# A message-passing layer: one tile in eighteen takes its source rows from x on chip, column by column, and not by a gather

## The chip, the cores and the metric

The kernel runs on one core of a Trainium2 chip. A core has five engines with a queue of instructions each: PE (matrix products), DVE (vector operations), ACT (activations and copies), POOL (here it only issues the gathers) and SP (issues DMAs). They run in parallel and wait for each other through semaphores; within a queue the order is fixed. PE, DVE and ACT work on 128 partitions of the on-chip memory; a product is accumulated in PSUM. The metric is the device time of one execution in microseconds (us), smaller being better; the median of several executions counts.

## The reference

One graph layer with a residual and a normalisation, on 12,500 nodes of 64 features and 200,000 edges of 32 features, all float32. The edges are sorted by `dst`; `src` is random.

```python
def _mlp(x, W1, b1, W2, b2):
    return jax.nn.relu(x @ W1 + b1) @ W2 + b2
msg_in = jnp.concatenate([nodes[row], nodes[col], edge_features], axis=-1)   # 64 + 64 + 32
messages = _mlp(msg_in, mW1, mb1, mW2, mb2)                                  # 160 -> 128 -> 64
aggregated = jax.ops.segment_sum(messages, col, num_segments=nodes.shape[0])
upd_in = jnp.concatenate([nodes, aggregated], axis=-1)
return _mlp(upd_in, uW1, ub1, uW2, ub2)                                      # 128 -> 128 -> 64
...
x = _layernorm(x + _L0_gnn_ref(x, src, dst, ...), axis=-1)
```

`row` is `src` and `col` is `dst`. The part of this page is the hidden layer of the message: relu(x[src] W1a + x[dst] W1b + e W1c + b1), where W1a, W1b and W1c are the three row blocks of mW1.

## The kernel before

**Tables.** x[src] W1a depends on the node alone. So the kernel first multiplies all of x with W1a and with W1b (plus b1) and writes two tables of 12,544 x 128 floats to HBM: A (`tab_a`, `chunk_a`) and B (`tab_b`, `chunk_b`). For an edge the hidden layer is then a row of A at its source, plus a row of B at its destination, plus the edge's own part.

**Tiles and groups.** 128 edges are a tile; there are 1563. Six tiles (`SUB`) are a group, s; there are 261. Twelve tiles, two groups, (`SUP`) share the selection matrices. The loop from line 583 handles group s in each turn and issues for several groups ahead.

**What a group needs.**
- `gather` (line 157): POOL issues one indirect DMA a tile (line 168). It fetches 128 rows of 512 bytes of A, at the indices in `src_s`, into one of 18 buffers `xg` (`ROWB`). So POOL runs up to 18 groups ahead and waits until DVE has read the buffer it wants (`frees`). The first ten groups (`XG`) gather rows of x instead, which PE transposes and multiplies with `w1a` (lines 231 and 270), since A is not ready yet.
- `windows` (line 217): the edges are sorted by destination, so a tile's destinations lie within 32 neighbouring nodes. SP loads six values from `wint` into registers (line 224) and issues six DMAs, each of 32 rows of B at a register's offset, into `rhs` (line 229).
- `loadd` and `load` (lines 177 and 211): SP loads the destinations (line 184) and the edge features (line 215) of two groups into `l`.
- `select` (line 187): DVE turns the destinations into zeros and ones that pick rows of the window (line 196), and into `sel`, which sums the edges into nodes (line 200).
- `edge_part` (line 246): PE multiplies [edge features; selection] with [W1c; window of B] in one product a tile (line 256), two passes each.
- `node_part` (line 260): DVE adds the gathered rows to the product (line 276), ACT applies the relu (line 277).
- `collect` (line 287): PE multiplies the result with the selection, at a column offset from a register (loaded at line 298), which sums the edges by node (line 302); a second product counts the edges (line 307).

At 33 points, 47 groups apart at first and four at the end, a block of nodes is complete: `update`, `residual`, `norm` and `store` (lines 333 to 370) compute the second layers and the normalisation and write the output. `rest` (line 504) issues some loads of the first groups; `columns` (line 326) loads x of a block of nodes.

**Order.** It is written out by hand. In turn s each engine gets, in this order: the gathers that have become possible, `windows(s + 2)`, `node_part(s)`, `collect(s - 1)`, in even turns `select` and `load`, in odd turns `loadd`, then `edge_part(s + 1)`. So in ACT's queue the relu of group s + 1 stands behind all that ACT gets in turn s, and on DVE the add at line 276 of group s + 1 stands behind the selections of turn s. The matrix products of group s + 1 stand on PE behind `collect(s - 1)`, which waits for the relu of group s - 1.

Of the kernel before, what the change touches and what calls it, by code (L numbers as in the profile page):

```python
# [10 lines left out]
F32 = mybir.dt.float32  # L11
I32 = mybir.dt.int32
AF = mybir.ActivationFunctionType
ALU = mybir.AluOpType
AX = mybir.AxisListType
ET = mybir.EngineType

P = 128
N, D, DE, DH = 12500, 64, 32, 128
E = 200000  # L20
EPS = 1e-5
NB = -(-N // P)
NPAD = NB * P
NT = -(-E // P)
SUB = 6
SUP = 12
NSUP = -(-NT // SUP)
NTP = NSUP * SUP
EPAD = NTP * P
NSUB = -(-NT // SUB)  # L30
# [7 lines left out]
XG = 10  # L38
# [2 lines left out]
EARLY = NCH * P  # L41
GE = 26
BS = 11
UB = 4
NCOL = (-(-N // P) + UB) * P
UN = 448
# [17 lines left out]


@with_exitstack
def gnn_kernel(ctx: ExitStack, tc: tile.TileContext, x1T, x, eT, e_rows, src, dst, dst_row, wrow, wnext, whalf,
               mW1, mb1, mW2, mb2, uW1, ub1, uW2, ub2, out):

# [20 lines left out]
    nc = tc.nc  # L92
    const = ctx.enter_context(tc.tile_pool(name="const", bufs=1))
# [7 lines left out]
    K = len(UPD)  # L101

    src_s = const.tile([P, NT], I32, name="src_s")
    wint = const.tile([1, NTP], I32, name="wint")
    past = const.tile([1, 1], F32, name="past")

    xall = const.tile([P, -(-NB // NCH), HB * P], F32, name="xall")
# [8 lines left out]
    w1a = const.tile([P, DH], F32, name="w1a")  # L116
# [19 lines left out]
    slot = cps[:, :WIN]  # L136
# [1 line left out]
    flag_i = const.tile([1, 1], I32, name="flag_i")  # L138
    usup = const.tile([1, K], I32, name="usup")
    ustep = const.tile([1, K], I32, name="ustep")  # L140
    woff = const.tile([1, NTP], I32, name="woff")
    wh = const.tile([P, NTP // 2], I32, name="wh")
    wa = const.tile([SUP, NSUP], I32, name="wa")
    wb = const.tile([SUP, NSUP], I32, name="wb")
# [9 lines left out]
    def tiles(s):  # L154
        return range(s * SUB, min((s + 1) * SUB, NT))

    def gather(s):

        if s >= XG or s % 2 == 0:
            buf = rows.tile([P, SUB, DH], F32, name="xg")  # L160
        else:
            buf = xg[s - 1][0]
        if s < XG:
            a = buf.rearrange("p k (b d) -> p (k b) d", d=D)[:, s % 2 * SUB:(s % 2 + 1) * SUB, :]
        else:
            a = buf.rearrange("p (b k) d -> p k b d", b=2)
        for i, t in enumerate(tiles(s)):
            nc.gpsimd.indirect_dma_start(  # L168
                out=a[:, i, :] if s < XG else a[:, i // 2, i % 2, :], out_offset=None, in_=A[:, :] if s >= XG else x[:, :],
                in_offset=bass.IndirectOffsetOnAxis(ap=src_s[:, t:t + 1], axis=0))  # L170
        xg[s] = buf, a

    with tc.tile_pool(name="sup", bufs=2) as sup, tc.tile_pool(name="work", bufs=2) as work, tc.manual_schedule():
# [66 lines left out]
        def parts(n):  # L240

            if n == SUB:
                return [(slice(0, 2), SUB // 2)]
            return [(slice(b, b + 1), (n - b + 1) // 2) for b in range(2) if n > b]

        def edge_part(s):

            n = len(tiles(s))
            g, j = divmod(s, SUP // SUB)

            pc = psum.tile([P, 2, 4, DH], F32, name="pc")[:, :, :SUB // 2]
            for i in range(n):
                k, b = divmod(i, 2)
                q, m = 64 * b, j * SUB // 2 + k

                nc.tensor.matmul(pc[:, b, k, :], L[g][q:q + 64, m, :], rhs[g % 2][q:q + 64, m, :],  # L256
                                 start=s >= XG or k == 0, stop=s >= XG)
            pcs[s] = pc

        def node_part(s):  # L260

            n = len(tiles(s))
            pc = pcs.pop(s)
            h = work.tile([P, 2, SUB // 2, DH], F32, name="h")
            if s < XG:
                xt = xs.pop(s)
                for i in range(n):
                    k, b = divmod(i, 2)
                    q = 64 * b
                    nc.tensor.matmul(pc[:, b, k, :], xt[q:q + 64, k, :], w1a[q:q + 64], start=False,  # L270
                                     stop=i + 2 >= n)
                nc.scalar.activation(h, pc, AF.Relu)
            else:
                a = xg.pop(s)[0].rearrange("p (b k) f -> p b k f", b=2)
                for b, m in parts(n):
                    nc.vector.tensor_tensor(h[:, b, :m], pc[:, b, :m], a[:, b, :m], op=ALU.add)  # L276
                    nc.scalar.activation(h[:, b, :m], h[:, b, :m], AF.Relu)  # L277
            hs[s] = h

        def opened(u):  # L280
# [37 lines left out]
        def close(u):  # L318

            ps, pn = sums.pop(u)  # L320
            nc.scalar.copy(sums_s[u % 2], ps)  # L321
            nc.scalar.copy(xw[u % 2][0:1, :UW], pn)

        us = {}

# [15 lines left out]
        def residual(u):  # L341

            n0 = us[u]
            py = psum.tile([P, UB, D], F32, name="py", tag="pc")
            for i in range(UB):
# [29 lines left out]
        def relative(a, b):  # L375

            wbc = work.tile([P, WCH], I32, name="wbc", tag="tb")
            nc.sync.dma_start(dst_s[:, a:b], dst[:, a:b])
            nc.sync.dma_start(wbc[:, :b - a], wrow[:, a:b].broadcast_to([P, b - a]))
            nc.vector.tensor_tensor(drc[:, a:b], dst_s[:, a:b], wbc[:, :b - a], op=ALU.subtract)  # L380
# [43 lines left out]
        def chunk_b(c, into):  # L424
            pb, tb = products(c, w1b)
            n = min(NCH, NB - c)
            pf, tf = (t.rearrange("p h i f -> p (h i) f")[:, :n] for t in (pb, tb))
            nc.vector.tensor_tensor(tf, pf, b1.unsqueeze(1).broadcast_to([P, n, DH]), op=ALU.add)
            for v in into:
                nc.sync.dma_start(v[:, c:c + n, :], tf)  # L430
# [53 lines left out]
        for k, c in enumerate(range(0, NB, NCH)):  # L484
# [14 lines left out]
            if k == 9:  # L499
                select(0)  # L500
                load(0)
                counts(0)

        def rest(s):

            if s == 1:
                relative(8 * SUP, 8 * SUP + WCH)
            elif s == 2:
                relative(8 * SUP + WCH, NT)
                halves(4 * SUP, NTP // 2)  # L510
            elif s == BS:
                nc.sync.dma_start(wa, wrow.rearrange("o (p c) -> (o p) c", c=NSUP))
                nc.sync.dma_start(wb, wnext.rearrange("o (p c) -> (o p) c", c=NSUP))
                nc.scalar.dma_start(w2, mW2)
                nc.scalar.dma_start(u1a, uW1[D:2 * D, :])
                nc.scalar.dma_start(b2c, mb2.rearrange("(f o) -> f o", o=1))
                nc.vector.memset(uz[:D], 0.0)
                nc.vector.memset(ux[:D], 0.0)
                nc.vector.memset(eps, EPS)
                nc.vector.memset(ones, 1.0)  # L520
                nc.vector.tensor_copy(ux[D:], ident[D:, D:])
                nc.scalar.dma_start(uz[D:], uW1[0:D, :])
                nc.scalar.dma_start(ux[ONE:ONE + 1], ub2.rearrange("(o f) -> o f", o=1))
                nc.scalar.dma_start(ub1_s, ub1.rearrange("(f o) -> f o", o=1))
                nc.scalar.dma_start(u2, uW2)
            elif s == BS + 2:
                weights()
                checks()
# [54 lines left out]
        for s in range(last + 3):  # L583
            g, j = divmod(s, SUP // SUB)
            while gathered < NSUB and frees(gathered) < s:
                gather(gathered)
                gathered += 1
            if s - 2 in due:
                norm(due[s - 2])
            if s + 2 < NSUB:  # L590
                windows(s + 2)
            if s < NSUB:
                node_part(s)
            if 1 <= s <= NSUB:
                collect(s - 1)
            if s + 1 in due:
                close(due[s + 1])
            if j == 0 and g + 1 < NSUP:
                select(g + 1)
                load(g + 1)  # L600
                counts(g + 1)
            if j == 1 and g + 2 < NSUP:
                loadd(g + 2)
            if chunks and s >= BS and chunks[0] < NCH + NB * (s + 1 - BS) / (SUP // SUB * (GE - 1) - BS):
                chunk_b(chunks.pop(0), [Bv])
            if s + 1 < NSUB:
                if s + 1 < XG:
                    transpose(s + 1)
                edge_part(s + 1)
            if s in due and due[s] + 1 < K:  # L610
                carry(due[s] + 1)
            if s in due:
                update(due[s])
            if s - 1 in due:
                residual(due[s - 1])
            if s + 2 in due:
                columns(due[s + 2])
            rest(s)
            if s - 2 in due:
                store(due[s - 2])  # L620
# [3 lines left out]
                          skip_runtime_bounds_check_because="a count of edges")  # L624
    with tc.If(flag > 0), tc.tile_pool(name="gen", bufs=1) as up:
# [28 lines left out]
        with tc.For_i(0, NT, 1) as t:  # L654
# [26 lines left out]
            pc = psum.tile([P, DH], F32, name="pcg", tag="pc")  # L681
# [4 lines left out]
            h = up.tile([P, DH], F32, name="hg")  # L686
# [6 lines left out]
            m = up.tile([P, 1], F32, name="m")  # L693
# [22 lines left out]
        with tc.For_i(0, NB, 1) as c:  # L716
# [24 lines left out]
            o = up.tile([P, D], F32, name="o")  # L741
# [45 lines left out]
```

## Time and profile before

| | us |
|---|---|
| median of 6 runs | 2753.09 (2743.26 to 2767.78) |
| the profiled execution, its own time | 2757.78 |
| its span in the profile | 2756.0 |
| gathers of A: issuing time on POOL, 1503 instructions | 1417.9 |
| edge products (line 256), 3126 passes on PE | 575.2 |
| collecting products (line 302), 3126 passes on PE | 685.3 |
| DVE, the add of the gathered rows (line 276), 252 | 238.8 |
| ACT, the relu (line 277), 252 | 210.9 |

A row of the profile's groups reads: line, engine, operation, what it writes <- what it reads, count | busy time, mean duration in ns | idle time of the engine before it, and what ended most of that. "issue" means that nothing the profile shows was waited for. SPq, PEldq and the like are instructions of an engine's sequencer (register loads, waits, DMA issues), which do not count as busy. In the order of time a line begins with the start and the length in us, and merges like instructions that follow each other.

### The profile page before, as it was taken

To read this page: it belongs to the slowest core of one execution; us is meant where nothing else is said; L and a number is where in the kernel's file an instruction comes from. 1 tells how busy PE (TensorE), PEld (TensorE's weight loads), DVE (VectorE), ACT (ScalarE), POOL (GpSimd) and SP (SyncE) were. 2 spreads that over 40 slices of the span, in tenths; PEclk is the share of its full clock that TensorE was granted. 3 is DMA by queue.
4 is the path that set the end of the run, shared out by engine and by line. 5 is a ranking of instruction groups with operands and counts; after the bars stand their busy time and mean duration, and the time that the engine had idled before them with its cause. 6 is when DMAs were issued, how large, how long until landed. Compare 5 with 4: busy or idle time off the path is not lost. (4 is left out here: it accounts for less than half of the span.)

```text
span 2756.0 us, 34854 instructions
## 1 busy us (share of the span) xinstructions
PE 1651.5 (60%) x9218; PEld 1410.1 (51%) x9218; DVE 551.7 (20%) x1165; ACT 359.0 (13%) x550; POOL 1475.7 (54%) x1572
## 2 busy tenths in 40 slices
PE   1413556666656565656666565665656575676798
PEld 1312555555555455545555554554555464564576
DVE  0200122221212112112212112121222122121233
ACT  0100111111111111111111111111111111111122
POOL 7175455656555656565655555555555555556400
PEclk7555555555555555555555555555555555555555
DMA  5421233333222222222222222222223222222221
GB/s 122 125 74 49 67 80 86 87 98 83 75 71 70 76 73 73 70 74 72 76 75 75 71 66 74 75 75 72 75 73 78 74 74 74 75 77 71 73 58 44
DMA packets 244062, 208.45 MB, mean 76 GB/s; under 512 B 78232, under 2 KB 208369, under 8 KB 243874
## 3 DMA queue, kind: packets, MB, share of 16 engines
q0 software_dynamic: 50016, 100.57, 14.7%
q1 hardware_dynamic: 179312, 96.69, 12.7%
q10 hardware_dynamic: 14546, 8.93, 1.1%
q8 instruction: 88, 1.44, 0.2%
q14 instruction: 100, 0.82, 0.1%
HBM read 188.25 MB, written 17.69 MB: 75 GB/s over the span
## 5 line engine op out<-in xcount | busy, mean ns | idle before, releaser
L168 POOL DMA_INDIRECT xg<-tab_a,src_s x1503 | 1417.9, 943 | 1128.2 <-issue 415.1
L256 PE MATMUL pc<-rhs,l 64*128 64x128 f32 x3126 | 575.2, 444 | 737.6 <-DMA l<-in_eT 441.8
L256 PEld LDWEIGHTS pc<-rhs,l 64*128 64x128 f32 x3126 | 457.2, 312 | 815.1 <-issue 658.6
L302 PEld LDWEIGHTS sums<-sel,h 128*128 128x128 f32 x3126 | 670.6, 318 | 158.3 <-issue 141.5
L302 PE MATMUL sums<-sel,h 128*128 128x32 f32 x3126 | 685.3, 386 | 93.8 <-issue 81.2
L276 DVE TENSOR_TENSOR h<-pc,xg 128x768 f32<-128x768 f32 x252 | 238.8, 949 | 990.0 <-issue 684.6
L277 ACT ACTIVATE h<-h 128x768 f32<-128x768 f32 x252 | 210.9, 837 | 876.6 <-DVE h L276 617.8
L196 DVE TENSOR_TENSOR l<-l,cps 128x768 f32<-128x768 int32 (+1 forms) x134 | 127.9, 954 | 545.1 <-DMA l<-in_dst_row 509.9
L208 ACT CAST selb<-sel 128x384 bf16<-128x384 f32 x131 | 66.7, 509 | 742.7 <-remote 262.2
L307 PE MATMUL cnt<-selb,one 128*1 128x32 bf16 x1563 | 96.7, 188 | 61.6 <-issue 61.3
L200 DVE TENSOR_TENSOR sel<-cps,drc 128x384 f32<-128x384 f32 x131 | 72.1, 550 | 237.0 <-remote 167.6
L307 PEld LDWEIGHTS <-one 128*1 128x1 bf16 x1563 | 58.1, 83 | 114.2 <-issue 99.5
L346 PE MATMUL py<-ux,xw 128*128 128x64 f32 x264 | 78.1, 394 | 5.7 <-ACT hTu L339 4.7
L347 PE MATMUL py<-u,hTu 128*128 128x64 f32 x264 | 76.7, 388 | 2.2 <-issue 1.6
L410 PE MATMUL pb<-w1a,xall 64*128 64x128 f32 x196 | 25.3, 432 | 85.1 <-DVE tb L418 59.5
L351 DVE BATCH_NORM_STATS2 st<-py 128x6 f32<-128x64 f32 x132 | 20.6, 218 | 258.6 <-PE py L347 231.8
L346 PEld LDWEIGHTS py<-ux,xw 128*128 128x128 f32 x264 | 63.9, 297 | 13.9 <-issue 7.1
L410 PEld LDWEIGHTS pb<-w1a,xall 64*128 64x128 f32 x196 | 22.6, 324 | 87.4 <-DVE tb L418 61.3
L168 POOL DMA_INDIRECT xg<-in_x,src_s x60 | 56.8, 946 | 19.2 <-issue 18.0
L347 PEld LDWEIGHTS py<-u,hTu 128*128 128x128 f32 x264 | 65.1, 301 | 2.0 <-issue 1.3
L337 PE MATMUL pu<-sums_s,w2u 128*128 128x448 f32 x66 | 61.5, 1035 | 0.5 <-ACT sums_s L321 0.5
L338 PE MATMUL pu<-xw,uz 128*128 128x448 f32 x66 | 55.1, 938 | 0.0
(87 smaller groups left out, 440.4 us busy)
## 6 DMA issues: line engine op xcount, KB each, us to landing
l<-in_dst_row SPq DMA_DIRECT2D x262, 96.0 KB
l<-in_eT SPq DMA_DIRECT2D x262, 96.0 KB
rhs<-tab_b SPq DMA_DIRECT2D x1563, 16.0 KB
xg<-tab_a,src_s POOLq DMA_INDIRECT x1503
tab_b<-tb SPq DMA_DIRECT2D x13, 512.0 KB
tab_a<-tb ACTq DMA_DIRECT2D x12, 512.0 KB
out<-o SPq DMA_DIRECT2D x33, 128.0 KB
xw<-in_x1T SPq DMA_DIRECT2D x33, 113.8 KB
```

What stands on the lines that cost most here:

```text
L168: nc.gpsimd.indirect_dma_start(out=a[:, i, :] if s < XG else a[:, i // 2, i % 2, :], out_offset=None, in_=A[:, :] if s >= XG else x[:, :], ...
L196: nc.vector.tensor_tensor(l[r], l[r].bitcast(I32), node[r].unsqueeze(2).broadcast_to([r.stop - r.start, SUP // 2, P]), op=ALU.is_equal)
L200: nc.vector.tensor_tensor(s[:, :nt], slot.unsqueeze(1).broadcast_to([P, nt, WIN]), drc[:, g * SUP:g * SUP + nt].unsqueeze(2).broadcast_to( ...
L208: nc.scalar.copy(sb[:, :nt], S[g][:, :nt])
L256: nc.tensor.matmul(pc[:, b, k, :], L[g][q:q + 64, m, :], rhs[g % 2][q:q + 64, m, :], start=s >= XG or k == 0, stop=s >= XG)
L276: nc.vector.tensor_tensor(h[:, b, :m], pc[:, b, :m], a[:, b, :m], op=ALU.add)
L277: nc.scalar.activation(h[:, b, :m], h[:, b, :m], AF.Relu)
L302: nc.tensor.matmul(ps[:, bass.ds(ws[i], WIN)], h[:, i % 2, i // 2, :], S[g][:, k0 + i, :], start=False, stop=ends and i == n - 1)
L307: nc.tensor.matmul(pn[:, bass.ds(ws[i], WIN)], one, SB[g][:, k0 + i, :], start=False, stop=ends and i == n - 1)
L337: nc.tensor.matmul(pu, w2u, sums_s[u % 2][:, :UN], start=True, stop=False)
L346: nc.tensor.matmul(py[:, i], xw[u % 2][:, i * P:(i + 1) * P], ux, start=True, stop=False)
L347: nc.tensor.matmul(py[:, i], hT[:, i * P:(i + 1) * P], u2, start=False, stop=True)
```

## The change

In one of each three groups from group 20 on, the sixth tile is no longer gathered. The kernel now keeps x, transposed, on chip (`xcol`: 64 partitions, a column of 12,544 nodes), loaded by seven DMAs in turns 3 to 9 (`rest`). For each of the 128 edges of such a tile, one instruction copies the 64 values of its source's column into a column of a 128-column tile `xo`. The column's offset comes from a register, which is loaded from `srow`, a table of the sources of these tiles. The copies are spread over three turns (`copies`, called before `edge_part(s + 1)`): of 42 or 43 columns a turn, ACT copies 24, by two register loads of twelve, and DVE the rest, as an addition of a PSUM value that is zero. PE then multiplies `xo` with `w1a` into the tile's product. In `node_part` of such a group the add covers five of six tiles, and the relu is two instructions: one of the sixth tile from PSUM, one of the rest. `wint` and `woff` now lie in the unused partition 0 of `xcol`.

```diff
+CG = 3
+CF = 6 * CG
+CA = 24
+    def copied(s):
+        return s >= CF and s % CG == CG - 1 and len(tiles(s)) == SUB
     def gather(s):
...
-        for i, t in enumerate(tiles(s)):
+        for i, t in enumerate(tiles(s)[:SUB - copied(s)]):
...
     def edge_part(s):
...
+                c = copied(s) and i == n - 1
                 nc.tensor.matmul(pc[:, b, k, :], L[g][q:q + 64, m, :], rhs[g % 2][q:q + 64, m, :],
-                                 start=s >= XG or k == 0, stop=s >= XG)
+                                 start=s >= XG or k == 0, stop=s >= XG and not c)
+                if c:
+                    nc.tensor.matmul(pc[:, b, k, :], xo[s // CG % 2][q:q + 64], w1a[q:q + 64], start=False, stop=True)
...
     def node_part(s):
...
+                if copied(s):
+                    for b, m in ((0, SUB // 2), (1, SUB // 2 - 1)):
+                        nc.vector.tensor_tensor(h[:, b, :m], pc[:, b, :m], a[:, b, :m], op=ALU.add)
+                    hf = h.rearrange("p b k f -> p (b k) f")
+                    nc.scalar.activation(hf[:, SUB - 1], pc[:, 1, SUB // 2 - 1], AF.Relu)
+                    nc.scalar.activation(hf[:, :SUB - 1], hf[:, :SUB - 1], AF.Relu)
...
+        def copies(s):
+            q, i = divmod(s + 2, CG)
+            t = q * CG + CG - 1
+            if t < CF or not t < NSUB or not copied(t):
+                return
+            k, e = i * P // CG, (i + 1) * P // CG
+            r = q - CF // CG
+            to = xo[q % 2]
+            def by_dve(o, i):
+                nc.vector.tensor_tensor(o, i, slot[D:, 0:1], op=ALU.add)
+            parts = []
+            for a, b, en, copy in ((k, k + CA // 2, ET.Activation, nc.scalar.copy),
+                                   (k + CA // 2, k + CA, ET.Activation, nc.scalar.copy),
+                                   (k + CA, e, ET.DVE, by_dve)):
+                _, v = nc.values_load_multi_w_load_instructions(
+                    srow[r:r + 1, a:b], engines=[en], min_val=0, max_val=N - 1,
...
+                parts += [(copy, a + i, v[i]) for i in range(b - a)]
+            for copy, i, v in parts:
+                copy(to[D:, i:i + 1], xcol[D:, bass.ds(v, 1)])
...
         def rest(s):
+            if 3 <= s and (s - 3) * XCH < NB * P:
+                c = (s - 3) * XCH
+                e = min(c + XCH, NB * P)
+                nc.sync.dma_start(xcol[D:, c:e], x1T[1:, c:e])
...
+                nc.sync.dma_start(srow, src_row[CF * SUB + SUB * CG - 1::SUB * CG, :][:NCT])
...
+            copies(s)
             if s + 1 < NSUB:
```

More of the change, by code (lines that the diff above doesn't have):

```diff
@@ L43 @@
 BS = 11
+CG = 3
+CF = 6 * CG
+CA = 24
+NCT = -(-(NSUB - CF) // CG)
 UB = 4
@@ L66, in gnn_kernel @@
 @with_exitstack
-def gnn_kernel(ctx: ExitStack, tc: tile.TileContext, x1T, x, eT, e_rows, src, dst, dst_row, wrow, wnext, whalf,
+def gnn_kernel(ctx: ExitStack, tc: tile.TileContext, x1T, x, eT, e_rows, src, src_row, dst, dst_row, wrow, wnext, whalf,
                mW1, mb1, mW2, mb2, uW1, ub1, uW2, ub2, out):
@@ L103, in gnn_kernel @@
     src_s = const.tile([P, NT], I32, name="src_s")
-    wint = const.tile([1, NTP], I32, name="wint")
+    xcol = const.tile([P, NB * P], F32, name="xcol")
+    wint, woff = (xcol[0:1, k * NTP:(k + 1) * NTP].bitcast(I32) for k in range(2))
+    srow = const.tile([NCT, P], I32, name="srow")
+    xo = [const.tile([P, P], F32, name=f"xo{k}") for k in range(2)]
     past = const.tile([1, 1], F32, name="past")
@@ L140, in gnn_kernel @@
     ustep = const.tile([1, K], I32, name="ustep")
-    woff = const.tile([1, NTP], I32, name="woff")
     wh = const.tile([P, NTP // 2], I32, name="wh")
@@ L274, in node_part @@
                 a = xg.pop(s)[0].rearrange("p (b k) f -> p b k f", b=2)
-                for b, m in parts(n):
-                    nc.vector.tensor_tensor(h[:, b, :m], pc[:, b, :m], a[:, b, :m], op=ALU.add)
-                    nc.scalar.activation(h[:, b, :m], h[:, b, :m], AF.Relu)
+                if copied(s):
[4 more added lines that the diff above has]
+                    nc.scalar.activation(hf[:, :SUB - 1], hf[:, :SUB - 1], AF.Relu)
+                else:
+                    for b, m in parts(n):
+                        nc.vector.tensor_tensor(h[:, b, :m], pc[:, b, :m], a[:, b, :m], op=ALU.add)
+                        nc.scalar.activation(h[:, b, :m], h[:, b, :m], AF.Relu)
             hs[s] = h
@@ L322, in close @@
             nc.scalar.copy(xw[u % 2][0:1, :UW], pn)
+        def copies(s):
[14 more added lines that the diff above has]
+                    srow[r:r + 1, a:b], engines=[en], min_val=0, max_val=N - 1,
+                    skip_runtime_bounds_check_because="sources are node numbers")
+                parts += [(copy, a + i, v[i]) for i in range(b - a)]
+            for copy, i, v in parts:
+                copy(to[D:, i:i + 1], xcol[D:, bass.ds(v, 1)])
         us = {}
@@ L502, in gnn_kernel @@
                 counts(0)
+        XCH = 2048
         def rest(s):
+            if 3 <= s and (s - 3) * XCH < NB * P:
+                c = (s - 3) * XCH
+                e = min(c + XCH, NB * P)
+                nc.sync.dma_start(xcol[D:, c:e], x1T[1:, c:e])
             if s == 1:
@@ L769 @@
         "src": sp.reshape(-1, P).T[:, :NT],
+        "src_row": sp.reshape(-1, P),
         "dst": dp[:EPAD].reshape(-1, P).T[:, :NT],
```

## The prediction

> **What bounds the kernel now.** I read the table of busy time first, to see whether one engine is full.
>
> ```profile
> PE 1651.5 (60%) x9218; PEld 1410.1 (51%) x9218; DVE 551.7 (20%) x1165; ACT 359.0 (13%) x550; POOL 1475.7 (54%) x1572
> ```
>
> None is. ACT and DVE, which get the new work, are the idlest. Next the pace, from the stages view over the even middle of the run (engines in the order PE, PEld, DVE, ACT, POOL; then granted clock, DMA share, GB/s):
>
> ```profile
> 500.00:2500.00 2000.00, 1241.35 (x6771) 1060.39 (x6770) 406.02 (x824) 266.97 (x404) 1141.88 (x1211) 0.51 0.29 75
> ```
>
> 1211 gathers are 201.8 groups of six, so a group takes 2000/201.8 = 9.91 us. ACT works 1.32 us of that and DVE 2.01 us. Then the order of time, for POOL and for SP's queue:
>
> ```profile
> 1504.65 3.12 SPq L229 DMA_DIRECT2D rhs<-tab_b  x6
> 1506.51 0.94 POOL L168 DMA_INDIRECT xg<-tab_a,src_s  x1 [4.10 <-DVE cps L194]
> 1507.76 0.94 POOL L168 DMA_INDIRECT xg<-tab_a,src_s  x1 [0.31 <-issue]
> ...
> 1509.95 13.44 SPq L229 DMA_DIRECT2D rhs<-tab_b  x6
> ...
> 1520.25 0.94 POOL L168 DMA_INDIRECT xg<-tab_a,src_s  x1 [0.30 <-issue]
> ...
> 1525.75 3.09 SPq L229 DMA_DIRECT2D rhs<-tab_b  x6
> ...
> 1535.00 0.94 POOL L168 DMA_INDIRECT xg<-tab_a,src_s  x1 [13.81 <-DVE cps L194]
> ```
>
> Gathers start 1.25 us apart (1506.51 to 1507.76), mostly twelve in a row. The six window loads of a group take SP 3.1 us when no gather runs, and 13.4 us while gathers flow, from about 3.4 us after a run's start to 2.2 us after its end: SP nearly halts. The engines that need SP's loads then wait, and POOL in its turn waits for a buffer that DVE frees late. The list of waits confirms both directions:
>
> ```profile
> DVE l L196 <- DMA l<-in_dst_row: 509.9, 98, 12.3
> PE pc L256 <- DMA l<-in_eT: 441.8, 78, 13.3
> POOL xg L168 <- DVE h L276: 326.3, 77, 10.4
> POOL xg L168 <- DVE cps L194: 286.8, 57, 16.0
> ```
>
> So gathers and the rest take turns. PE's clock (0.51) matters little: PE idles 38% here. PE too is halted late in a run of gathers, one instruction at a time, for no reason the trace names:
>
> ```profile
> 1549.15 0.28 PEld L256 LDWEIGHTS pc<-rhs,l 64*128 64x128 f32 x1 [1.12 <-issue]
> 1549.85 0.37 PE L256 MATMUL pc<-rhs,l 64*128 64x128 f32 x1 [1.04 <-issue]
> ```
>
> Whether ACT and DVE are halted as well this trace cannot tell: they issue only a handful of instructions in such a stretch.
>
> **What is removed.** Copied tiles are those of groups 20, 23, ... 257: 80 gathers of 1563. At 1.25 us that is 100 us at most (if the gather runs set the pace) and 0 at least (if SP's own issuing does).
>
> **What is added.** The copies are spread over 240 groups: 128 columns per three groups, of which ACT takes 24 in each group and DVE 18.67 on average. No row shows such an instruction; the nearest are these (durations in ns: least, median, greatest):
>
> ```profile
> L355 ACT ACTIVATE sd<-mv,eps x33: 297/297/298, 703.4 to 2750.1; 128x4 f32<-128x4 f32 x33
> L298 PEldq TENSOR_LOAD <-woff x261: 776/1124/1806, 132.7 to 2737.6; - x131
> L312 PEldq TENSOR_LOAD <-ustep x32: 302/308/321, 689.3 to 2725.5; - x32
> L307 PEldq FUSED_REGOPS  x1563: 37/37/37, 134.6 to 2741.8; - x196
> 109.63 0.13 DVE L445 COPY usup<-wint 1x1 int32<-1x1 int32 x1
> ```
>
> ACT, per group:
> - Copies: a small ACT instruction lasts 0.297 us, and neighbours overlap by 0.10 (L277 at 1514.74 starts 0.53 us after L339, which lasts 0.63). That is 0.20 from start to start, and 24 x 0.20 = 4.80 us. The register operation ahead of each (0.037 us) hides under the copy before it; uncovered it would be 0.9 us.
> - Register loads: one value takes 0.308 us, six take 1.124 (median), so a further value costs 0.163. Twelve values take 0.308 + 11 x 0.163 = 2.10 us, two such loads 4.20. They stand ahead of all the copies, so ACT runs dry behind them. By the least of six values (0.776) it would be 2 x 1.34 = 2.68; if ACT's queue covers them wholly, 0. I take the medians, because a load in a crowded stretch is what happens here.
> - The relu of a copied group becomes two: by L355 (4 columns, 0.297) and L277 (768, 0.837), 0.39 + 0.75 less 0.10 of overlap is 0.2 more, every third group: under 0.10.
> - With its present 1.32 this makes 1.32 + 4.80 + 4.20 + 0.10 = 10.42 us, against a pace of 9.91. ACT becomes the engine that sets the pace.
>
> The Trainium skill's page "Runtime: NRT & Kernel Launch", section on instruction fetch, speaks against the change more strongly: about 200 ns for each register loaded. The slope between the two rows above is 163 ns. By the page's figure, an estimate, two loads of twelve would cost 4.8 us and ACT 11.0 us a group, some 145 us more over the run than by the rows.
>
> DVE, per group: 2.01 + one load of 18.67 values (0.308 + 17.67 x 0.163 = 3.19) + 18.67 copies x 0.17 (L445 to its successor at 109.80) = 3.17, in all 8.4 us, under the pace. But they come after the selection and ahead of the next L276, so that add, the relu behind it and the buffer it frees for POOL wait up to 6.4 us longer. Slack of 1.5 us a group hides them; without it they would cost the same as ACT's excess.
>
> PE: two passes more per copied tile, 160 matmuls at 0.18 (twelve take 2.1 us at 1525.54), 28 us, hidden in PE's idle time; 0 to 28, I take 0. Its new wait for the copied columns holds up the collecting matmuls behind it, but the copies are ordered one whole group earlier, so it costs nothing unless ACT falls a group behind.
>
> SP: eight more DMAs ahead of group 10. At about 0.4 us to issue (L330's median is 0.372) 3 us; the 3.2 MB at 158 GB/s (the best stage) 20 us if nothing hides it. SP's rows queue behind it. 0 to 23; I take 5, since the DMA share there is a quarter.
>
> **Sum.** ACT's excess 240 x (10.42 - 9.91) = 122 us, plus 5: 2757.8 + 127 = 2885. The removed 100 us are not subtracted, because POOL then waits for ACT's pace. The sum is against the profiled execution (2757.8, span 2756.0 plus 1.8 around it), 4.7 over the median of the six, 2753.1; I state 2885. Its own range: 2770 when half of the loads is covered, 3150 when ACT keeps half of its present wait for L276 (617.8/252 = 2.45 us, so 1.2 x 240 = 290 on top).
>
> **Rival: the copies are hidden, faster.** ACT's and DVE's idle time is 8.6 and 7.9 us a group, and their sequencers can load registers while the engine still works off its queue. Without the loads ACT needs 6.2 us, DVE 5.2. Then the full 100 us come out, less up to 28 for PE and SP: 2757.8 - 100 + 28 = 2686 (2660 to 2739). Against it: a relu then stands behind the copies in ACT's order, and the next collecting matmuls behind the relu.
>
> **Rival: ACT is halted as SP is, much slower.** SP passes the 24 instructions of six window loads in 13.4 us while gathers flow, 0.56 each, against 0.13 otherwise. ACT gets some 50 more instructions a group. (A window load is a register operation, a wait, a move and the DMA: the view of L229 has 1563 of each, 1538 of the wait.) Per pair of groups the halted stretch is about 12.6 us (11.33 gathers) and lets 22 of ACT's instructions through. With ACT's 20.8 us of work a pair this gives 20.8 + 12.6 - 22 x 0.19 = 29.2, or 14.6 a group: 3880. With the loads covered (12.4 us a pair, 0.12 an instruction) 22.4, or 11.2: 3065. I put it at 3350; it decides as soon as ACT loses over 1 us a group. For it: SP. Against it: PE, an engine with a datapath as ACT is, passes some fifty matmuls of a run before it is halted, and its register operations never take longer than 37 ns.
>
> **Rival: no change** (the gain and ACT's excess cancel): 2757.
>
> **How the numbers follow.** Forecast 0.40, hidden 0.27, halted 0.26, no change 0.07. A difference under 0.5% cannot be told from none. So faster 0.27, same 0.07, slower 0.66. The range 2660 to 3350 leaves out some 0.05 of the hidden case below it and 0.13 of the halted case above it; the forecast alone is 2770 to 3150.
>
> **What would show it.** The gather group must have 1423 instructions in place of 1503. ACT's copies should stand 0.2 us apart and its two loads take about 2.1 us each; a lone relu should show waits ended by its own engine's queue, and POOL's waits for L276 should grow. If copies stand 0.5 us or more apart while gathers flow, the halting rival is right; if POOL's waits shrink or stay and the pace falls to 9.5 us, the hidden one is. Loads near 1 us, or overlapped with copies, would make the forecast wrong.

## The result, and the profile after

| | before | after |
|---|---|---|
| median, us | 2758.69 (46 runs) | 2959.38 (20 runs, 2942.52 to 2978.74) |
| ratio | | 1.0732, 95% interval 1.0714 to 1.0750 |
| span of the profiled execution, us | 2756.0 | 2948.0 |
| time per group, 500 to 2500 us | 9.91 | 10.62 |

The change makes the kernel slower by 7.3%, 201 us. The table of busy time, the stages view of the even middle (engines as before: PE, PEld, DVE, ACT, POOL) and three groups of the changed kernel:

```profile
PE 1560.3 (53%) x9378; PEld 1337.7 (45%) x9378; DVE 1151.3 (39%) x5725; ACT 1023.0 (35%) x6390; POOL 1401.4 (48%) x1492
```

```profile
500.00:2500.00 2000.00, 1068.59 (x6402) 919.35 (x6402) 845.37 (x4327) 769.97 (x4965) 1005.80 (x1067) 0.52 0.26 68
```

```profile
L180 POOL DMA_INDIRECT xg<-tab_a,src_s x1423 | 1343.6, 944 | 1369.6 <-DVE h L298 424.2
L367 ACT COPY xo<-xcol 64x1 f32 x5760 | 662.0, 188 | 1208.9 <-issue 1206.5
...
L356 DVE TENSOR_TENSOR xo<-xcol,cps 64x1 f32<-64x1 f32 x4480 | 593.7, 159 | 831.7 <-issue 829.2
```

1423 gathers of A in place of 1503: the change does what it says. 1067 gathers in the stage, at 17 for three groups, are 188.3 groups: 2000/188.3 = 10.62 us each. 240 groups at 0.71 us more are 170 of the 201 us. By busy time no engine is full. But ACT stands idle for 1206 us, and DVE for 829, just ahead of copies, with "issue" as the reason. Register loads are not counted as busy, so this idle time is where they hide. The list of waits:

```profile
ACT xo L367 <- issue: 1206.5, 884, 6.3
DVE xo L356 <- issue: 829.2, 482, 4.6
POOL xg L180 <- DVE h L298: 424.2, 80, 14.2
...
POOL xg L180 <- DVE cps L206: 324.1, 76, 16.5
PEld pc L272 <- ACT xo L367: 278.9, 59, 12.0
...
POOL xg L180 <- DVE h L292: 138.1, 27, 10.7
```

POOL waits longer for the buffers that DVE frees (for the add, which is now two lines, 424 + 138 = 562 us; 326 before), and PE has a new wait, for ACT's copies. In the order of time, ACT alone:

```profile
1520.04 2.51 ACT L367 COPY xo<-xcol 64x1 f32 x24 [5.30 <-issue]
1522.57 0.84 ACT L299 ACTIVATE h<-h 128x768 f32<-128x768 f32 x1
1524.27 1.85 ACT L367 COPY xo<-xcol 64x1 f32 x17 [0.85 <-issue]
1526.68 0.19 ACT L367 COPY xo<-xcol 64x1 f32 x1 [0.56 <-issue]
1527.38 0.19 ACT L367 COPY xo<-xcol 64x1 f32 x1 [0.51 <-issue]
1528.13 0.19 ACT L367 COPY xo<-xcol 64x1 f32 x1 [0.56 <-issue]
1529.49 0.19 ACT L367 COPY xo<-xcol 64x1 f32 x1 [1.18 <-issue]
...
1537.24 0.28 ACT L294 ACTIVATE h<-pc 128x128 f32<-128x128 f32 x1 [4.70 <-issue]
```

Three things are to be seen. 5.30 us without work, most of it register loads, stand ahead of 24 copies. The 24 copies then take 2.51 us, 0.105 each; from start to start it is 0.101 in the median. And in the next group ACT falls, after 17 copies, into a beat of 0.70 us, or twice that, for each instruction, with nothing named that it waits for: the halting that SP and PE showed in the kernel before, now on ACT.

### The profile page after: what moved, and what is told of

It reads as the page before. It is cut to its first block, busy times and chain, and to the rows that moved or that the text cites. A ratio compares the mean times of both kernels' runs of the same rounds, so it can differ in the third digit from the quotient of the medians.

```text
span 2948.0 us, 56571 instructions
## 1 busy us (share of the span) xinstructions
PE 1560.3 (53%) x9378; PEld 1337.7 (45%) x9378; DVE 1151.3 (39%) x5725; ACT 1023.0 (35%) x6390; POOL 1401.4 (48%) x1492
## 4 chain that ended last, share of the span: by engine, by line
issue 32%; ACTq 19%; POOL 13%; ACT 11%; PE 8%; DVE 5%; another core or an unknown queue 5%; DMA 4%; DVEq 2%; SPq 1%; POOLq 0%
POOL xg L180 13%; ACTq L362 13%; ACT xo L367 8%; ACTq L367 5%; PE sums L324 3%; DMA xg<-tab_a,src_s 2%; PE pc L269 2%; DVEq L362 2%; DVE h L298 1%; DVE xo L356 1%; ACT selb L220 1%; DVE l L208 1%; DMA tab_a<-tb 1%; ACT h L299 1%
## 5 line engine op out<-in xcount | busy, mean ns | idle before, releaser
L180 POOL DMA_INDIRECT xg<-tab_a,src_s x1423 | 1343.6, 944 | 1369.6 <-DVE h L298 424.2
L367 ACT COPY xo<-xcol 64x1 f32 x5760 | 662.0, 188 | 1208.9 <-issue 1206.5
L356 DVE TENSOR_TENSOR xo<-xcol,cps 64x1 f32<-64x1 f32 x4480 | 593.7, 159 | 831.7 <-issue 829.2
L269 PE MATMUL pc<-rhs,l 64*128 64x128 f32 x3126 | 435.7, 434 | 195.5 <-DVE o L409 67.6
L269 PEld LDWEIGHTS pc<-rhs,l 64*128 64x128 f32 x3126 | 358.3, 314 | 220.5 <-issue 76.8
L298 DVE TENSOR_TENSOR h<-pc,xg 128x768 f32<-128x768 f32 (+1 forms) x172 | 163.1, 949 | 155.5 <-DMA xg<-tab_a,src_s 99.8
L272 PE MATMUL pc<-w1a,xo 64*128 64x128 f32 x160 | 60.8, 482 | 288.2 <-ACT xo L367 241.9
L299 ACT ACTIVATE h<-h 128x768 f32<-128x768 f32 (+1 forms) x172 | 143.6, 836 | 148.5 <-DVE h L298 75.5
L272 PEld LDWEIGHTS pc<-w1a,xo 64*128 64x128 f32 x160 | 40.5, 312 | 307.1 <-ACT xo L367 278.9
L292 DVE TENSOR_TENSOR h<-pc,xg 128x384 f32<-128x384 f32 (+1 forms) x160 | 71.1, 485 | 76.1 <-PE pc L272 67.8
L220 ACT CAST selb<-sel 128x384 bf16<-128x384 f32 x131 | 65.8, 502 | 98.7 <-DVE sel L212 40.2
```

The source lines that it names most:

```text
L180: nc.gpsimd.indirect_dma_start(out=a[:, i, :] if s < XG else a[:, i // 2, i % 2, :], out_offset=None, in_=A[:, :] if s >= XG else x[:, :], ...
L272: nc.tensor.matmul(pc[:, b, k, :], xo[s // CG % 2][q:q + 64], w1a[q:q + 64], start=False, stop=True)
L356: nc.vector.tensor_tensor(o, i, slot[D:, 0:1], op=ALU.add)
L367: copy(to[D:, i:i + 1], xcol[D:, bass.ds(v, 1)])
```

## The experiments

Three theories are tried, L for loads, H for halting, G for gathers. Theory L: the register loads are what fills ACT (and DVE). Their length depends on the column at which they start: in this trace a load of 12 values takes 0.80 us from columns 0 and 12 (bytes 0 and 48), and 2.64 from columns 42, 54, 85 and 97 (bytes 168, 216, 340, 388). The first two starts are multiples of 16 bytes, the others are not. Theory H: the halting is the cost, since ACT and DVE now have many small instructions that it can catch. Theory G: without either, the gathers, 1.25 us each, set the time.

The runs fell on chips of two kinds. On one kind the kernel before took 2810 us (and 2759 in the runs above); on the other, 1979 to 1981. Ratios are to the kernel before on the same chip. The table has the timed runs in their order; a rule stands between chips.

| kernel | before, us | this, us | ratio, 95% interval |
|---|---|---|---|
| aligned loads | 1979.44 | 1882.72 | 0.9505, 0.9489 to 0.9521 |
| loads only | 1979.44 | 1881.93 | 0.9506, 0.9490 to 0.9522 |
| copies of fixed columns | 1979.44 | 1882.34 | 0.9510, 0.9494 to 0.9525 |
| neither | 1979.44 | 1879.96 | 0.9495, 0.9479 to 0.9511 |
| --- | | | |
| the changed kernel | 2810.10 | 3039.49 | 1.0831, 1.0799 to 1.0863 |
| no gathers | 2810.10 | 2141.31 | 0.7621, 0.7606 to 0.7637 |
| loads, few copies | 2810.10 | 2847.20 | 1.0134, 1.0114 to 1.0154 |
| --- | | | |
| aligned loads, again | 1980.21 | 1882.79 | 0.9509, 0.9493 to 0.9525 |
| neither, again | 1980.21 | 1881.75 | 0.9503, 0.9487 to 0.9519 |
| --- | | | |
| aligned loads, third time | 1980.81 | 1882.14 | 0.9500, 0.9485 to 0.9516 |
| the changed kernel | 1980.81 | 2111.36 | 1.0664, 1.0638 to 1.0690 |

**Aligned loads.** The whole change, its columns cut at 0, 44 and 88, so that every load starts at a multiple of 16 bytes. ACT keeps its 24 columns a group; DVE gets 20, 20 and 16 in place of 18, 19 and 19.

```diff
-            k, e = i * P // CG, (i + 1) * P // CG
+            k, e = 44 * i, min(44 * i + 44, P)
```

> The whole change, with the columns cut at 0, 44 and 88 in place of 0, 42 and 85, so that each load begins at a multiple of 16 bytes. In the trace of the changed kernel the loads that begin so take 0.80 us on ACT and 1.6 on DVE, the others 2.64 and 4.4. If the place of the first value decides, all loads take 0.8 and 1.6, ACT saves 2.4 us a group and DVE 1.9. Theory of the loads: the pace falls by most of that, 2680 to 2800. Theory of the halting: the copies are still halted, 2900 or more.

Measured: 1882.72 us against 1979.44. The gathers in its trace:

```profile
L180 POOL DMA_INDIRECT xg<-tab_a,src_s x1423 | 1342.7, 944 | 436.9 <-issue 412.1
```

POOL has next to no wait left but its own pace: 1483 gathers x 1.25 = 1854 us, and some 29 around them, make the time. Loads and copies are hidden. What the alignment is worth could not be read here, since the changed kernel was not beside it.

**Loads only.** The loads as in the change, no copies; the copied columns of x are left at zero.

```diff
-            for copy, i, v in parts:
-                copy(to[D:, i:i + 1], xcol[D:, bass.ds(v, 1)])
```

> The register loads stay, the copies and their register operations are left out (the same x term is missing). Theory of the loads (ACT's two loads of twelve, 4.0 us a group in the trace of the changed kernel, and DVE's one of 18 or 19, 3.4 us, stand in order ahead of the relu and the add): most of the price stays, 2850 to 2920. Theory of the halting (copies let through one by one while gathers flow): three loads a group are too few to be halted, so within 1.5% of the run with neither.

Measured: 1881.93. This tells nothing of loads. The line of the loads (least, median and greatest duration in ns, then first and last start) in its trace:

```profile
L362 ACTq EVENT_SEMAPHORE  x480: 17/17/17, 187.3 to 1827.2; - x160
L362 DVEq EVENT_SEMAPHORE  x240: 21/21/21, 185.8 to 1826.2; - x120
```

Only waits are left: the loads fell out of the program, as nothing used their values. The run equals "neither", and the question went into a later one.

**Copies of fixed columns.** No loads; as many copies, from columns that are known beforehand and are not the sources'.

```diff
-            ...
+            parts = [(nc.scalar.copy if a < k + CA else by_dve, a, 97 * a % N) for a in range(k, e)]
             for copy, i, v in parts:
-                copy(to[D:, i:i + 1], xcol[D:, bass.ds(v, 1)])
+                copy(to[D:, i:i + 1], xcol[D:, v:v + 1])
```

> The copies stay but take fixed columns of x, so that no register is loaded (the x term of the sixth tile is then that of other nodes). Theory of the halting: ACT and DVE still issue 42 copies a group and are still let through one by one, so most of the price stays, 2850 to 2920, with copies 0.7 us or more apart in the flow of gathers. Theory of the loads: 24 copies at 0.105 us are 2.5 us on ACT, which its idle time hides: within 1.5% of the run with neither.

Measured: 1882.34. Copies alone are hidden on this chip.

**Neither.** No loads and no copies; 80 gathers fewer and the 160 products more stay.

```diff
-            parts = []
-            ...
-            for copy, i, v in parts:
-                copy(to[D:, i:i + 1], xcol[D:, bass.ds(v, 1)])
```

> The copies and their register loads are left out (xo stays zero, so the sixth tile of a copied group lacks its x term); the 80 gathers stay removed and the product with xo stays. It shows what the removal alone is worth. If the runs of gathers set the pace (they and the rest take turns), some 2670, that is 90 to 100 us under the kernel before (2759). If SP's own issuing sets it, within 1% of 2759. In both cases the rest up to 2959 is the price of the copies, 200 to 290.

Measured: 1879.96, 99 us less than the kernel before: 80 x 1.25 = 100, the whole of it. Up to here the chip had given theory G four times, and H and L no chance to show: the expectations of these four runs were written for a chip like the first, and their numbers could not be tested on this one.

**The changed kernel beside the kernel before, on another chip.** No edit.

> The changed kernel as it is, on the chip of this call. Theory G (where no engine is halted, the time is that of the gathers, 1.25 us each one after the other): 1483 x 1.25 + 27 = 1881 us beside 1979 for the kernel before, ratio 0.950, as the version with aligned loads measured. Theory L (the register loads from columns that are no multiple of 16 bytes make ACT the bound): per group 24 copies x 0.105 = 2.5, loads 4.0, its other work 1.4 and some 0.3 of issue, 8.2 us, against 5.67 gathers x 1.25 = 7.08, so 240 x 1.1 = 270 us more than 1881, about 2150, ratio 1.085. If this chip halts the engines while gathers run (the kernel before near 2759): about 2959, ratio 1.073.

> The kernel before, for its trace on this chip. If it takes about 1979 us: gathers 1.25 us apart from end to end, SP's six window loads about 3 us also while gathers run, and no row of instructions 0.70 us apart. If it takes about 2759: gaps of 3 to 8 us between the runs of gathers and SP at 0.70 us ticks, as in its first profile.

Measured: 3039.49 against 2810.10; the kernel before, run once more for its trace, took 2798.54. This chip halts. SP's queue in the kernel before, in the order of time:

```profile
1503.15 9.11 SPq L229 DMA_DIRECT2D rhs<-tab_b  x6
1513.67 0.72 SPq L215 DMA_DIRECT2D l<-in_eT  x2
1518.66 2.80 SPq L229 DMA_DIRECT2D rhs<-tab_b  x6
```

Six window loads take 2.80 us or 9.11, as in the first profile. ACT in the changed kernel:

```profile
1515.01 1.52 ACT L367 COPY xo<-xcol 64x1 f32 x14 [4.43 <-issue]
1517.06 0.19 ACT L367 COPY xo<-xcol 64x1 f32 x1 [0.52 <-issue]
1517.81 0.19 ACT L367 COPY xo<-xcol 64x1 f32 x1 [0.57 <-issue]
1518.51 0.19 ACT L367 COPY xo<-xcol 64x1 f32 x1 [0.51 <-issue]
```

The beat of 0.70 us again. Counted over the trace, 643 of the spacings between ACT's copies lie between 0.6 and 1.6 us, 656 us in all; in the first profile of the changed kernel 535, 519 us in all.

**No gathers.** On the same chip: the gathers of groups 10 to 260 are left out, and a buffer of zeros is read in place of what they bring. (The gather buffers go from 18 to 6; those lines are not shown.)

```diff
+            buf = xz
...
-        for i, t in enumerate(tiles(s)[:SUB - copied(s)]):
-            nc.gpsimd.indirect_dma_start(
+        if s < XG:
+            for i, t in enumerate(tiles(s)[:SUB - copied(s)]):
+                nc.gpsimd.indirect_dma_start(
```

> The change with the gathers of groups 10 to 260 left out (x taken as zero there). Theory G: what stays is PE's work, 1527 us busy at a granted clock of 0.54, so 1600 to 1750 us. Theory L: ACT's 8.2 us per group stay, 240 of them and the start, so 2100 to 2200, as long as with the gathers. Halting by the gathers: on a chip where the kernel before takes 2759, this kernel shows no ticks of 0.70 us and is at least 700 us shorter than the changed kernel.

Measured: 2141.31, ratio 0.7621, and 898 us under the changed kernel. ACT and then SP in the order of time, and the waits ahead of the copies (its lines are four further down):

```profile
1003.62 2.51 ACT L371 COPY xo<-xcol 64x1 f32 x24 [4.94 <-issue]
1006.16 0.84 ACT L303 ACTIVATE h<-h 128x768 f32<-128x768 f32 x1
1006.91 0.49 ACT L224 CAST selb<-sel 128x384 bf16<-128x384 f32 x1
...
1016.14 2.51 ACT L371 COPY xo<-xcol 64x1 f32 x24 [4.36 <-issue]
```

```profile
1007.96 3.09 SPq L245 DMA_DIRECT2D rhs<-tab_b  x6
```

```profile
ACT xo L371 <- issue: 802.8, 309, 6.2
DVE xo L360 <- issue: 637.3, 301, 4.5
```

Not one spacing of ACT's copies lies between 0.6 and 1.6 us any more, and SP takes 3.1 us for six windows (the median over the even middle; 4.7 at the most, against 6.7 and 15.6 in the changed kernel on this chip). So on this chip the halting comes with the gathers. What is left are blocks of copies behind 4 to 5 us of loads, on both engines, and a pace of 7.73 us a group that has nothing to do with gathers. Theory L's 2100 to 2200 held, theory G's 1600 to 1750 fell.

**Loads, few copies.** On the same chip: each load as in the change, but only the first of its copies, 3 a group in place of 42.67.

```diff
-                parts += [(copy, a + i, v[i]) for i in range(b - a)]
+                parts += [(copy, a, v[0])]
```

> The change with its loads at the same columns, but only the first copy of each load (3 in place of 42.67 per group; the other columns are left at zero). Theory L: ACT then has loads 4.0 and other work 1.7, 5.7 us, DVE 3.4 and 2.3, both under 7.08, so the gathers set the pace again: 1882 us where the kernel before takes 1979. A rival that the loads themselves delay what is behind them on ACT and DVE whatever their sum: over 1950. On a chip that halts: G has no say; loads alone would then be the rise over the version without loads and copies.

Measured: 2847.20, 37 us over the kernel before and 192 under the changed one. The loads are whole here:

```profile
L362 ACTq TENSOR_LOAD <-srow x480: 773/2628/3901, 377.2 to 2801.1; - x160
L362 DVEq TENSOR_LOAD <-srow x240: 1570/4294/5176, 375.8 to 2796.9; - x120
```

So on a chip that halts, and with the long loads in place, the other copies cost 192 of the changed kernel's 229 us. The loads, less what the removal of 80 gathers saves, make the other 37. How much the loads cost by themselves stays between 37 us, if the 80 gathers saved nothing there, and 37 + 80 x 2810/1563 = 181, if they saved their whole share.

**Aligned, and neither, again.** The question was what both give on a chip that halts.

> The aligned version again, on the chip of this call. Where the kernel before takes 1979 it gave 0.951. Where it takes about 2800 (a chip that halts the engines while gathers run): theory L (the loads' length is in the path: ACT's 4.0 us of loads per group become 1.6) expects up to 2.4 x 240 = 580 us less than the changed kernel where ACT is the bound throughout, and about 1.02 of the kernel before if loads and copies add their costs (1.083 less the 0.06 that the loads cost beside 0.95). Theory H (the halted copies are the cost and the loads hide in the halts) expects 1.06 to 1.08, as the changed kernel.

> The change without loads and copies (the copied columns of x are left at zero; 80 gathers fewer and 240 groups' extra multiplications stay), on the chip of this call. Where the kernel before takes 1979 it gave 0.950. Where it takes about 2800: if the 80 gathers' share of the pace is saved whole, 80 x 2810/1563 = 144 us, ratio 0.949, and then the loads (the version with few copies, 1.013) cost 0.064 and the copies (1.083) 0.070 more; if the time of a halting chip is set by the engines' halted work and not by the count of gathers, 0.98 to 1.00, and the loads cost 0.01 to 0.03 only.

Measured: 1882.79 and 1881.75 against 1980.21. It was a chip without halts, and the first ratios came again. What was expected for a halting chip was not tested.

**Aligned, and the changed kernel, on one chip.** The pair that tells L from G.

> The aligned version on one more chip, beside the changed kernel on the same. Where the kernel before takes 1979: 1882, ratio 0.951, for the third time. Where it takes about 2800 (chips that halt): theory L, the loads' length adds to the path of the halted engines, 0.97 to 1.04; theory H, the loads hide in the halts, 1.06 to 1.08.

> The changed kernel on the same chip. Where the kernel before takes 1979: theory G (gathers alone set the time) 1882, ratio 0.951; theory L 2130 to 2170, ratio 1.08 to 1.10: the version without gathers took 2141 with the same loads and copies, and ACT and DVE, not the gathers, would be what sets it. Where the kernel before takes about 2800: 1.073 to 1.083 again.

Measured: 1882.14 and 2111.36, against 1980.81. The one line that moves where the loads start is worth 229 us, and turns a loss of 6.6% into a gain of 5.0%. The loads of the changed kernel, and those of the aligned one:

```profile
L362 ACTq TENSOR_LOAD <-srow x480: 780/2633/4057, 185.5 to 2064.7; - x160
L362 DVEq TENSOR_LOAD <-srow x240: 1572/4301/5645, 184.0 to 2060.8; - x120
```

```profile
L362 ACTq TENSOR_LOAD <-srow x480: 768/793/1194, 185.3 to 1830.3; - x160
L362 DVEq TENSOR_LOAD <-srow x240: 1095/1356/1973, 183.8 to 1828.5; - x120
```

SP's queue and ACT in the changed kernel on this chip:

```profile
1513.39 3.11 SPq L241 DMA_DIRECT2D rhs<-tab_b  x6
1517.08 0.78 SPq L227 DMA_DIRECT2D l<-in_eT  x2
1519.45 3.09 SPq L241 DMA_DIRECT2D rhs<-tab_b  x6
```

```profile
1507.45 2.51 ACT L367 COPY xo<-xcol 64x1 f32 x24 [5.43 <-issue]
1509.99 0.30 ACT L400 ACTIVATE sd<-mv,eps 128x4 f32<-128x4 f32 x1
1512.59 0.84 ACT L299 ACTIVATE h<-h 128x768 f32<-128x768 f32 x1 [2.31 <-DVE h L298]
1514.77 2.51 ACT L367 COPY xo<-xcol 64x1 f32 x24 [1.34 <-issue]
```

No halts: SP takes 3.1 us for six windows, and no spacing of ACT's copies lies between 0.6 and 1.6 us. Yet with register loads and other sequencer work counted in, ACT is taken for 910 of the 1000 us from 500 to 1500, and DVE for 901; in the aligned version for 684 and 724. On the chips that halt, ACT comes to the same once the halted stretches count as taken: 819 of the 1000 us in the first profile of the changed kernel, 897 with the spacings of 0.6 to 1.6 us filled in; 812 and 902 in the second. What is held there is the register operation ahead of a copy; here are the first profile of the changed kernel and the one of this chip:

```profile
L367 ACTq FUSED_REGOPS  x5760: 3/46/1392, 374.8 to 2908.2; - x199
L367 ACTq FUSED_REGOPS  x5760: 46/46/52, 187.4 to 2070.0; - x199
```

On this chip a group takes 7.82 us (the mean from group 40 to 240), as without gathers on the other chip (7.73), where its gathers would need 17/3 x 1.25 = 7.08. Expected of L were 2130 to 2170, so its size was a little less; G's 1882 fell.

## Why the prediction was right, point by point

It said slower, 2885 us, with ACT as the engine that sets the pace, at 10.42 us a group. Measured were 2959 and 10.62. Direction and range held; the sum came close because errors cancelled. The direction hung on something that the prediction did not see, the columns at which the loads start: where nothing halts, the same change with other cuts is faster than the kernel before.

- **The bound before.** Gathers and the rest taking turns, with SP nearly halted, is right for the chip that was profiled, and the trace of the kernel before on another such chip shows it again. It is no property of the program: on three other chips the same kernel, not traced there, takes 1979 to 1981 us, of which 1563 gathers x 1.25 are 1954.
- **80 gathers fewer, 0 to 100 us.** 98.7 us come out where nothing halts and the loads are aligned. On a halting chip it was not measured alone.
- **ACT's copies, 24 x 0.20 = 4.80 us.** Mis-sized. They take 0.105 us each, 2.51 in all: a copy lasts 0.188 us, not 0.297, and its neighbour starts 0.101 after it, just past its middle.
- **ACT's loads, 4.20 us.** Measured 4.03 (967.9 us in 240 groups), but the working behind it was wrong. It took a price per value from the median of a row (0.776, 1.124 and 1.806 us for six values) that mixes two kinds. In that trace the loads of even groups, which start at a multiple of 16 bytes, take 0.82 us and those of odd groups 1.47 (medians); next to none takes 1.124. Four values from a multiple of 16 bytes take about 0.26 us together (on DVE in the aligned version 16 values take 1.12 and 20 take 1.38); otherwise one value takes 0.22 (12 in 2.64). Values left over from the fours are dear too: DVE's 18 aligned values take 1.61 us in the changed kernel, more than 20. Hardly a load of twelve takes the 2.1 us that was forecast: a third of them take about 0.80, near the 1 us that was named as a sign against the forecast, and the others about 2.64 (medians). That a median between two kinds fitted columns of which one third is aligned was luck. The Trainium skill's page "Runtime: NRT & Kernel Launch", in its section on instruction fetch, gives about 200 ns for each register loaded; by the page's list of terms these are loads from HBM. The loads here, from a table on chip, come near it where they are unaligned (0.22 us) and not where they are aligned (0.79/12 = 0.066 us).
- **The sum for ACT.** With the measured terms and no halts it is 1.32 + 2.51 + 4.03 + 0.10 = 8.0 us, and 7.82 were measured where nothing halts. That is closer than the working deserves: 242 us of the loads there, 1.0 us a group, run under ACT's other work, and ACT still waits for 90 of 1000 us. On the first chip the 535 halted copies take 519 us in place of 54, some 1.9 us a group more, which the forecast had left to a rival. Copies too dear by 2.3 us and halts missing by 1.9 nearly cancelled. The forecast's own range does not follow from its terms: with half of the loads covered ACT needs 8.32 us, under the pace, and the sum is 2763, not 2770; with 290 on top it is 3175, not 3150.
- **The halting rival.** Its mechanism is there: its own sign, copies 0.5 us or more apart while gathers flow, stands in the trace for about a tenth of them; without gathers the sign went, and without most copies 192 us went. Its price, 3065 us at the least, was too high. It let ACT pass 22 instructions through each halted stretch at SP's rate, for every pair of groups, and counted the loads as the copies; but of 5760 copies only some 535 came out at the halted beat, and a load is one instruction: its median is 2.63 us with halts and without.
- **The hidden rival** is what the aligned version does where nothing halts. What spoke against it in the change as it is was the length of the loads, not a lack of idle time on ACT and DVE.
- **DVE, 8.4 us and under the pace.** Measured 2.01 + 3.43 + 18.67 x 0.129 = 7.8 us. Where nothing halts DVE is about as full as ACT (901 for 910 of 1000 us). No run tells which of the two sets the pace; the chain that ended last has 17% of the span in ACT's loads and 2% in DVE's. On the first chip DVE's lateness shows in POOL's longer wait for the add, as was foreseen (562 us for 326).
- **PE's new wait, free unless ACT falls a group behind.** It was not free: PE's weight loads waited 59 times for the copies, 279 us, in the first profile.
- **SP's eight loads, 5 us,** were not tried alone. (The best stage of the kernel before moves 164 GB/s, not 158; the term stays about 20 us at the most.)

Three things stay open: why some chips halt the engines while gathers run and others don't, whether ACT or DVE sets the pace of the changed kernel, and what the aligned version gives on a chip that halts. It beats both kernels on a chip where all three ran, by 5% and 11% (1882.14 of 1980.81 and of 2111.36), but on a halting chip it wasn't measured. The 192 us that the copies cost there were measured beside the long loads; whether they stay beside short ones belongs to that question.

## What to carry to other kernels

Count register loads as time of their engine, though the table of busy time leaves them out: look for idle time that ends with "issue" ahead of instructions with register offsets, then for the loads' own row, and see whether its least and greatest are two kinds. Load register values in fours, from addresses that are multiples of 16 bytes (the addresses alone were worth 229 of 2111 us where nothing halted). And ask whether a stall in a profile belongs to the program or to the chip it ran on: the same kernel took 1980 us on some and 2800 on others, and what is worth doing to it differs.

## What the runs showed of the hardware

- The length of a register load from the on-chip memory depends on its address: 12 values on ACT take 0.79 to 0.80 us from a multiple of 16 bytes, and 2.63 to 2.69 from 4 or 8 bytes past one (medians by column), with and without gathers in flight, on both kinds of chip.
- On two chips, or on one met twice, the instructions of SP and ACT leave at a beat of about 0.70 us, or twice that, for stretches in which gathers are in flight: in the two traces of the changed kernel 535 and 643 spacings of ACT's copies lie between 0.6 and 1.6 us, and 159 and 173 of DVE's. PE shows it in rows of the kernel before, 0.70 us apart. Without gathers the chip of the second trace has no such spacing among the copies of either engine.
- On a chip that does not halt, the changed kernel has no such spacing either, and in the aligned version all gathers of A run about 1.25 us apart, none over 1.4.
- Small copies on ACT (64x1) last 0.188 us but start 0.101 us apart with a register's offset, and 0.091 with a fixed one (medians).
